# Turning the weighted LoRA projections: TensorE transposes, or VectorE block transposes with ScalarE copies

## The chip, the core and the metric

The kernel runs on one core of a Trainium2 chip. The metric is the device time of one execution in microseconds (us). The engines are named as the profile names them: PE is TensorE's matmul, PEld its weight load, DVE is VectorE, ACT is ScalarE, POOL is GpSimd and SP is SyncE, which issues nearly all DMAs here.

## What is computed

There are 8 samples of 256 tokens and 1024 features, all fp32. Each sample picks one of 8 conditioning matrices, and the result runs through a linear layer with a routed low-rank (LoRA) correction:

```
y      = einsum('bsi,boi->bso', x, weight[adapter_ids])        # 1024 x 1024 per sample
base   = einsum('btd,od->bto', y, base_W) + base_b
probs  = softmax(einsum('btd,nd->btn', y, router_W) + router_b) # n = 15
topk_p, topk_i = top_k(probs, 8);  mapped = expert_map[topk_i]
w      = weight of each of the 8 experts for each token
h      = einsum('btd,erd->bter', y, A)                          # 8 experts x rank 16 = 128
out    = x + base + einsum('bter,eor->bto', h * w[..., None], B) * 2.0
```

The product `h * w` is what the change is about. For one sample it is 256 tokens by 128 expert-rank values. The code calls it `hw`. It is computed with tokens on the partitions, and the last product (`B`) needs it with the 128 expert-rank values on the partitions: it has to be turned.

## The kernel before

**Two stages.** Stage one (lines 251 to 534) makes `y` for one sample after another, 8 rounds of its loop (`b` = 0 to 7). Stage two (lines 539 to 812) makes base and correction for two groups of four samples. Both use a Strassen-like scheme with 7 block products in place of 8: three PSUM accumulators `pa`, `pb`, `pc` collect blocks of several products, with copies and sums in between. In stage one a block is 4 fp32 matmuls of 128x512 (`block`, line 276; the trace shows two passes for each, 8 records). In stage two the scheme is nested: 7 outer products (`seven`) with 7 inner blocks each, per group; `here` counts the outer products from 0 to 13. A block there is 4 matmuls of 128x256 (line 573) and, where the correction is added, 2 more with `hwT` (line 582).

**The order is written by hand.** PE, DVE, ACT and SP run what the code issues, in that order (`manual_schedule`). One round of stage one for a middle sample issues on PE:

- `pa` = a11 b11 (read by an ACT copy at line 452)
- `pb` = a12 b21 (read by DVE at line 457)
- the two transposes of the last round's `hw` (line 247)
- `pc` = s1 t1 (read by an ACT copy at line 482)
- `pa` += s2 t2 (read by an ACT copy at line 484)
- `pc` += s4 b22 (read by DVE at line 464)
- `pa` += the block with a21 (read by DVE at line 470), the projection of the sample before (line 139, `ph`), `pa` += a22 t4 (read by DVE at line 287)

(Counting the transposes out, these are blocks one to seven with the projection ahead of the seventh. In round 7 the order is another: `pa`, `pc` with s1 t1, `pa` with s2 t2, `pb`, the two transposes, then the block with a21, `pc` with s4 b22, and the last.)

The block s1 t1 and the block s4 b22 use the same accumulator `pc`, so the second of them may not write before the ACT copy of line 482 has read it.

**Turning y.** DVE transposes 32x32 blocks in place (`flip`, line 287), and 16 ACT copies (`moves`, line 298) carry 32 partitions each from one quarter of the partitions to another: source quarter `a`, target quarter `r`, `a` running fastest. There are two such sets of 16 per sample; the second one is called `behind` and runs at the start of the next round, 4 copies ahead of the ACT copy of line 452 and 12 behind it.

**The router and hw.** `project(b, ph)` issues 16 matmuls and returns small DVE and ACT steps: `logits`, `softmax`, `top`, `route_to` and `weigh` (line 197), which writes `hw`, one of two places by the sample's parity. In round `b` of stage one it serves sample `b - 1`.

**Turning hw.** `turn` (lines 243 to 248) is called once per sample: in rounds 2 to 7 behind the `pb` block (line 460), and in stage two behind the outer products `here` = 1 and 2 (lines 806 and 812). It issues two PE transposes with an identity into a PSUM tile `pt` and one ACT copy of 128x256 into `hwT` (line 248). The first four samples' `hwT` is first used by the outer product 1, the others' by product 8.

**The head.** Line 421 issues 11 matmuls of the identity with itself into the same `pt`, before the first weights arrive. The pools of PSUM are `ps_t` (1 bank, `pt`), `ps` (6 banks) and `ps_h` or `ps_e` (1 bank).

Of the kernel before, what the change touches and what calls it, by code (L numbers as in the profile page):

```python
# [10 lines left out]
F32 = mybir.dt.float32  # L11
# [17 lines left out]
def kernel(  # L29
# [15 lines left out]
    nc = tc.nc  # L45
    P = 128
    B = ids.shape[1]
    S = 256
    KC = 8
    KH = 4  # L50
    OH = 512
# [5 lines left out]
    GB = 4  # L57
    NTT = S // P
# [4 lines left out]
    wpool = ctx.enter_context(tc.tile_pool(name="w", bufs=8))  # L63

    tpool = ctx.enter_context(tc.tile_pool(name="t", bufs=6))
    ps_t = ctx.enter_context(
        tc.tile_pool(name="ps_t", bufs=1, space=bass.MemoryType.PSUM)
    )
    dram = ctx.enter_context(
        tc.tile_pool(name="scratch", bufs=1, space=bass.MemoryType.DRAM)  # L70
    )
# [12 lines left out]
    ident = const.tile([P, P], F32, name="ident")  # L84
# [9 lines left out]
    hwTs = [const.tile([P, 2, 2, S], F32, name=f"hwT{g}") for g in range(B // GB)]  # L94
# [37 lines left out]
    def project(b, ph, order=(0, 1)):  # L132


        y = yv[b // GB]
        th, bi = b % GB // 2, b % 2
        for j in order:
            for k in range(KC):
                nc.tensor.matmul(  # L139
                    ph[:, j, : ER + N],  # L140
                    lhsT=y[:, k // KH, th, k % KH // 2, bi, k % 2, ts(j, P)],
                    rhs=ar_sb[:, k, :],
                    start=(j == order[0] and k == 0),
                    stop=(k == KC - 1),
                    skip_group_check=True,
                )
        t = places
        hw = t[f"hw{b % 2}"]

        def logits():  # L150
            lg = t["lg"]
            nc.vector.tensor_add(
                lg, ph[:, :, ER : ER + N], rb.unsqueeze(1).to_broadcast([P, NTT, N])
            )
            mx = t["mx"]
            nc.vector.tensor_reduce(mx, lg, AX.X, ALU.max)
            nc.vector.tensor_sub(lg, lg, mx.unsqueeze(2).to_broadcast([P, NTT, N]))
            nc.scalar.activation(t["ex"], lg, AF.Exp)
            nc.scalar.copy(t["h"], ph[:, :, :ER])

        def softmax():
            den = t["den"]
            nc.vector.tensor_reduce(den, t["ex"], AX.X, ALU.add)
            rden = t["rden"]
            nc.vector.reciprocal(rden, den)
            pr = t["pr"]
            nc.vector.tensor_mul(pr, t["ex"], rden.unsqueeze(2).to_broadcast([P, NTT, N]))

        def top():
            pr, first = t["pr"], t["top"]  # L170
            rest = t["rest"]
            for j in range(NTT):
                nc.vector.max(out=first[:, j, :], in_=pr[:, j, :])
            for j in range(NTT):
                nc.vector.match_replace(
                    out=rest[:, j, :],
                    in_to_replace=first[:, j, :],
                    in_values=pr[:, j, :],
                    imm_value=0.0,
                )  # L180

            nc.vector.tensor_sub(t["kept"], pr, rest)

        w = t["w"]

        def route_to(j):
            def run():
                kr = t[f"kr{j}"]
                nc.vector.tensor_mul(
                    kr, route, t["kept"][:, j, :].unsqueeze(1).to_broadcast([P, E, N])  # L190
                )
                nc.vector.tensor_reduce(w[:, j, :], kr, AX.X, ALU.add)

            return run

        def weigh():
            nc.vector.tensor_mul(
                hw.rearrange("p j (e r) -> p (j e) r", r=R),
                t["h"].rearrange("p j (e r) -> p (j e) r", r=R),
                w.rearrange("p j e -> p (j e)").unsqueeze(2).to_broadcast(  # L200
                    [P, NTT * E, R]
                ),
            )

        return [logits, softmax, top, route_to(0), route_to(1), weigh], (b, hw)

# [33 lines left out]

    EN = mybir.EngineType

    def turn(b, hw):

        pt = ps_t.tile([P, S], F32, name="pt")
        for j in range(NTT):
            nc.tensor.transpose(pt[:, ts(j, P)], hw[:, j, :], ident)  # L247
        nc.scalar.copy(hwTs[b // GB][:, b % GB // 2, b % 2, :], pt)


    with ExitStack() as phase:
        xpool = phase.enter_context(tc.tile_pool(name="x", bufs=2))
        prep = phase.enter_context(tc.tile_pool(name="prep", bufs=1))
        ps = phase.enter_context(
            tc.tile_pool(name="ps", bufs=2, space=bass.MemoryType.PSUM)
        )
# [25 lines left out]
                    skip_group_check=True,  # L282
                )

        def flip(half, of):

            nc.vector.transpose(half, of)  # L287

        def moves(b, oh, m):


# [10 lines left out]
                for r in range(4)  # L302
                for a in range(4)
            )

        def run(steps, n=None):
            for _ in range(len(steps) if n is None else min(n, len(steps))):
                steps.popleft()()

        spare = prep.tile([P, 28, P], F32, name="spare")  # L310

# [104 lines left out]
        x, q = load(0)  # L416
        first = q

        idle = ps_t.tile([P, S], F32, name="pt")
        for _ in range(11):  # L420
            nc.tensor.matmul(idle[:, :P], lhsT=ident, rhs=ident, start=True, stop=True)
        t1, t2, t4 = turns(x)
        first_sum(q)
# [3 lines left out]
        waiting = None  # L427
        behind = deque()
        for b in range(B):
# [16 lines left out]
            pb = ps.tile([P, OH], F32, name="pb")  # L446
# [8 lines left out]
            def first_results():  # L455
                block(pb, q["a12"], b21, True)
                nc.vector.tensor_add(m0[:, 0], pb, m0[:, 0])
                flip(m0[:, 0], m0[:, 0])
                if waiting:
                    turn(*waiting)  # L460

            def by_s4():
                block(pc, q["s4"], b22, False)
# [29 lines left out]
            elif not last:  # L493
# [11 lines left out]
                steps, waiting = project(b - 1, ph)  # L505
# [6 lines left out]
            else:  # L512
# [12 lines left out]
                steps, waiting = project(b - 1, ph)  # L525
# [13 lines left out]
    with ExitStack() as phase:  # L539
# [9 lines left out]
        ps = phase.enter_context(  # L549
            tc.tile_pool(name="ps", bufs=2, space=bass.MemoryType.PSUM)  # L550
        )
# [121 lines left out]
        for g in range(B // GB):  # L673
            y, hw = yv[g], hwTs[g]
# [75 lines left out]
            for n, (right, base, into, done, *up_hw) in enumerate(seven):  # L750
                here = g * len(seven) + n
                gaps = {k: [] for k in range(7)}

                if n + 1 < len(seven):
                    follows = seven[n + 1][0]
                else:
                    follows = None if end else yv[g + 1][:, 0, 0]
                steps = [] if follows is None else differences(follows)
                nexts = []


                def advance(n, steps=steps, nexts=nexts):
                    def run():
                        soon.extendleft(
                            (lambda s=s: nexts.append(s())) for s in reversed(steps[n])
                        )

                    return run


                steps = [steps[:2], steps[2:3], steps[3:]]
                for k, m in ((0, 0), (3, 1), (4, 2)):
                    gaps[k].append(advance(m, steps))
                if here == 0:
                    gaps[2].append(lambda: soon.extend(steps_of))
                if n == 0:
                    gaps[1].append(lambda: first_terms((0, 0), (0, 1)))
                    gaps[4].append(lambda: first_terms((1, 0)))
                    gaps[6].append(lambda: first_terms((1, 1)))
                elif n in outer:  # L780
                    gaps[1].append(lambda n=n: soon.extend(outer[n]))
                if n in result_of:
                    for k, ij in enumerate([(0, 0), (1, 1), (0, 1), (1, 0)]):
                        gaps[k].append(lambda r=result_of[n] + ij: load_x(*r))
                if end and n == 6:

                    r = (1, 0, 1, 0)
                    gaps[5].append(
                        lambda: soon.append(lambda: add(u[:, 1, 0], u[:, 1, 0], xs[r]))
                    )  # L790
                if here == 0:
                    for k, count in enumerate((0, 1, 1, 4, 4, 4, 2)):
                        gaps[k].append(lambda count=count: run(behind, count))
                if here + 2 < len(lefts):

                    def fetch(m=here + 2):
                        left[m] = load_left(lefts[m])

                    gaps[5].append(fetch)
                product(  # L800
                    left.pop(here), terms, right, base, into, done, gaps, *up_hw,
                    *([None] * (2 - len(up_hw))), end and n == 6
                )
                terms = nexts
                if here == 1:
                    turn(*waiting)

                    ph = ps_e.tile([P, 2, S], F32, name="pe")
                    steps, waiting = project(B - 1, ph)
                    soon.extend(steps)  # L810
                elif here == 2:
                    turn(*waiting)


# [63 lines left out]
```

## Time and profile before

| what | value |
|---|---|
| median of 3 runs (lowest to highest) | 435.49 us (434.95 to 435.57) |
| the profiled execution, its own time | 435.61 us |
| its span, first to last instruction | 433.8 us |
| PE busy | 428.2 us, 99% of the span |
| PEld busy | 294.7 us, 68% |
| DVE busy | 325.7 us, 75% |
| ACT busy | 138.7 us, 32% |
| TensorE clock granted over the span | 1.00 |
| transposes of line 247 | 16 (2 for each of 8 samples) |
| copies of line 248 | 8, 0.372 us each |
| copies of line 298 | 256, 0.402 us each |

The table is an average over two stages with different loads: in the four rounds from 66.6 to 179.3 us PE is busy all the time, DVE 23.2 us of 28.2 and ACT 15.8 us of 28.2. In stage two ACT has little to do. The chain of waits follows the work that ended last backwards; its lines give start, length, engine and tile. The timelines give for each group of instructions the start, the length, the line, the operation, and in brackets how long the engine idled before it and what ended that.

### The profile page before, as it was taken

The page shows a single profiled execution, that of the slowest core. Times are in us where ns is not written, and L with a number is a line of the kernel's source. Part 1 is how long each engine was busy: PE and PEld are TensorE (multiplying, and loading weights), DVE is VectorE, ACT ScalarE, POOL GpSimd, SP SyncE. Part 2 cuts the span into 40 slices and gives each one's busy share as a digit, 9 for nine tenths or more (in the row PEclk, how much of TensorE's full clock was granted, in tenths as well). Part 3 has the DMA queues.
Part 4 walks back from the last instruction along what each step waited for, and adds up shares of the span by engine and source line. Part 5 has one row for each costly group of instructions (what it writes and reads, how often), then busy time and mean ns, then how long its engine had stood idle before and what let it go on. Part 6 is the DMA issues. An engine that isn't in the chain of part 4 may idle for free.

```text
span 433.8 us, 4826 instructions
## 1 busy us (share of the span) xinstructions
PE 428.2 (99%) x1654; PEld 294.7 (68%) x1654; DVE 325.7 (75%) x548; ACT 138.7 (32%) x338; POOL 0.7 (0%) x6
## 2 busy tenths in 40 slices
PE   8999999999999999999999999999999999999997
PEld 5344454644646446455458898888888888888886
DVE  0699999886878888988886866946597858745595
ACT  1019276662755636736538300000201200000200
POOL 0000000000000000000000000000000000000000
PEclk9999999999999999999999999999999999999999
DMA  7997997859578698891749565522968725912843
GB/s 255 417 366 258 348 338 272 329 231 313 200 289 289 219 336 295 290 306 60 259 199 371 214 208 206 196 96 91 380 216 275 286 68 201 391 58 63 299 163 128
DMA packets 32778, 106.04 MB, mean 244 GB/s; under 512 B 3058, under 2 KB 6898, under 8 KB 29554
## 3 DMA queue, kind: packets, MB, share of 16 engines
q1 hardware_dynamic: 32610, 105.21, 66.7%
q10 hardware_dynamic: 144, 0.52, 0.4%
q8 instruction: 13, 0.21, 0.2%
q14 instruction: 11, 0.09, 0.1%
HBM read 84.49 MB, written 21.23 MB: 244 GB/s over the span
## 4 chain that ended last, share of the span: by engine, by line
PE 96%; DMA 2%; SPq 1%; issue 0%; DVE 0%
PE pa L276 24%; PE pa L573 22%; PE pc L276 13%; PE pc L573 11%; PE pb L276 7%; PE ph L139 6%; PE pb L573 6%; PE pc L582 3%; DMA wt<-in_wq_dram 2%; PE pb L582 2%; PE pa L582 1%; PE pe L139 1%; PE pe L573 1%; PE pt L247 0%; SPq L353 0%; DMA ids_sb<-in_ids_dram 0%
## 5 line engine op out<-in xcount | busy, mean ns | idle before, releaser
L298 ACT COPY y<-late 32x256 f32<-32x256 f32 x256 | 103.0, 402 | 63.2 <-DVE late L287 60.2
L573 PE MATMUL pa<-tt,wt 128*128 128x256 f32 x324 | 78.0, 379 | 0.0
L573 PEld LDWEIGHTS pa<-tt,wt 128*128 128x128 f32 x324 | 61.4, 190 | 8.7 <-DVE q L603 0.3
L276 PE MATMUL pa<-wt,x 128*128 128x512 f32 x128 | 57.7, 593 | 0.6 <-DMA wt<-in_wq_dram 0.6
L276 PE MATMUL pa<-wt,tt 128*128 128x512 f32 x120 | 54.0, 593 | 0.0
L276 PEld LDWEIGHTS pa<-wt,x 128*128 128x128 f32 x128 | 24.1, 190 | 30.7 <-issue 29.9
L276 PEld LDWEIGHTS pa<-wt,tt 128*128 128x128 f32 x120 | 22.3, 190 | 26.1 <-issue 25.9
L612 ACT ACTIVATE q<-pa,bb 128x256 f32<-128x256 f32 x12 | 5.0, 470 | 105.9 <-PE pa L573 105.0
L139 PEld LDWEIGHTS ph<-late,y 128*128 128x128 f32 x224 | 28.4, 189 | 3.3 <-issue 3.3
L276 PE MATMUL pb<-wt,x 128*128 128x512 f32 x64 | 29.1, 595 | 0.6 <-DMA wt<-in_wq_dram 0.6
L276 PE MATMUL pc<-wt,x 128*128 128x512 f32 x64 | 28.9, 594 | 0.0
L276 PE MATMUL pc<-wt,tt 128*128 128x512 f32 x64 | 28.8, 592 | 0.0
L139 PE MATMUL ph<-late,y 128*128 128x143 f32 x224 | 28.6, 284 | 0.0
L573 PE MATMUL pc<-tt,wt 128*128 128x256 f32 x112 | 27.8, 379 | 0.0
L399 DVE TENSOR_TENSOR wt<-wt 128x2048 f32<-128x2048 f32 (+1 forms) x9 | 18.4, 2049 | 8.5 <-PE pa L276 5.9
L573 PE MATMUL pc<-y,wt 128*128 128x256 f32 x96 | 24.0, 379 | 0.0
L573 PE MATMUL pb<-y,wt 128*128 128x256 f32 x96 | 24.0, 379 | 0.0
L276 PEld LDWEIGHTS pb<-wt,x 128*128 128x128 f32 x64 | 12.0, 190 | 16.6 <-issue 14.3
L573 PEld LDWEIGHTS pc<-tt,wt 128*128 128x128 f32 x112 | 21.3, 190 | 2.9
L276 PEld LDWEIGHTS pc<-wt,x 128*128 128x128 f32 x64 | 12.1, 190 | 15.5 <-issue 14.8
L573 PE MATMUL pa<-y,wt 128*128 128x256 f32 x92 | 21.8, 379 | 0.0
L276 PEld LDWEIGHTS pc<-wt,tt 128*128 128x128 f32 x64 | 11.7, 190 | 12.9 <-issue 12.2
(120 smaller groups left out, 531.2 us busy)
## 6 DMA issues: line engine op xcount, KB each, us to landing
wt<-in_wq_dram SPq DMA_DIRECT2D x28, 1024.0 KB, 5.6
wt<-left_raw SPq DMA_DIRECT2D x14, 1024.0 KB, 5.3
wt<-left_sum SPq DMA_DIRECT2D x14, 768.0 KB, 8.4
out_dram<-q SPq DMA_DIRECT2D x31, 256.0 KB, 2.3
x<-in_xq_dram SPq DMA_DIRECT2D x7, 1024.0 KB, 7.0
late<-in_xr_dram SPq DMA_DIRECT2D x20, 256.0 KB, 6.6
wt<-in_wq_dram SPq DMA_DIRECT2D x8, 512.0 KB, 7.8
spare<-in_bq_dram SPq DMA_DIRECT2D x4, 1024.0 KB, 5.3
```

The source lines that it names most:

```text
L139: nc.tensor.matmul(ph[:, j, : ER + N], lhsT=y[:, k // KH, th, k % KH // 2, bi, k % 2, ts(j, P)], rhs=ar_sb[:, k, :], start=(j == order[0] ...
L276: nc.tensor.matmul(acc, lhsT=right[:, k, :], rhs=left[:, k, :], start=(first and k == 0), stop=(k == KH - 1), skip_group_check=True,)
L298: lambda a=a, r=r: nc.scalar.copy(y[32 * r : 32 * r + 32, :, :, a, :], m[32 * a : 32 * a + 32, :, :, r, :])
L399: nc.vector.tensor_add(q["s1"][:, h], q["a21"][:, h], q["a22"][:, h])
L573: nc.tensor.matmul(acc[mi][:, mi, :], lhsT=left[:, 2 * k + mi, :], rhs=right[:, k, :], start=(first and k == 0 and (mi == 0 or acc[0] is n ...
L582: nc.tensor.matmul(acc[mi][:, mi, :], lhsT=up[:, ts(mi, P)], rhs=hw, start=False, stop=True, skip_group_check=True,)
L612: nc.scalar.activation(dst[:, mi], acc[mi][:, mi], AF.Identity, bias=bb[:, c : c + 1])
```

## The change

`turn` no longer uses PE or PSUM. `weigh` gets one more DVE instruction: a transpose of 32x32 blocks of `hw` in place (128x256). `turn` then returns 16 ACT copies of 32 partitions by 2x32 elements, in the same order of quarters as the copies of line 298, and its callers run them all at the places where the transposes and the one copy were issued. The pool `ps_t` goes; the identity matmuls of the head write into a `pb` tile of the pool `ps`, and there are 13 of them in place of 11. `flip` and `run` move out of stage one's block, without change.

```diff
-    ps_t = ctx.enter_context(
-        tc.tile_pool(name="ps_t", bufs=1, space=bass.MemoryType.PSUM)
-    )
...
                     [P, NTT * E, R]
                 ),
             )
+            flat = hw.rearrange("p j f -> p (j f)")
+            flip(flat, flat)
...
+    def flip(half, of):
+
+        nc.vector.transpose(half, of)
+
+    def run(steps, n=None):
+        for _ in range(len(steps) if n is None else min(n, len(steps))):
+            steps.popleft()()
+
     def turn(b, hw):
 
-        pt = ps_t.tile([P, S], F32, name="pt")
-        for j in range(NTT):
-            nc.tensor.transpose(pt[:, ts(j, P)], hw[:, j, :], ident)
-        nc.scalar.copy(hwTs[b // GB][:, b % GB // 2, b % 2, :], pt)
+        to = hwTs[b // GB][:, b % GB // 2, b % 2].rearrange("p (j a t) -> p j a t", j=NTT, a=4)
+        return deque(
+            (
+                lambda a=a, r=r: nc.scalar.copy(
+                    to[32 * r : 32 * r + 32, :, a, :],
+                    hw[32 * a : 32 * a + 32, :, ts(r, 32)],
+                )
+            )
+            for r in range(4)
+            for a in range(4)
+        )
...
-        idle = ps_t.tile([P, S], F32, name="pt")
-        for _ in range(11):
+        idle = ps.tile([P, OH], F32, name="pb")
+        for _ in range(13):
             nc.tensor.matmul(idle[:, :P], lhsT=ident, rhs=ident, start=True, stop=True)
...
                 if waiting:
-                    turn(*waiting)
+                    run(turn(*waiting))
...
                 if here == 1:
-                    turn(*waiting)
+                    run(turn(*waiting))
...
                 elif here == 2:
-                    turn(*waiting)
+                    run(turn(*waiting))
```

More of the change, by code (lines that the diff above doesn't have):

```diff
@@ L283, in block @@
                 )
-        def flip(half, of):
-            nc.vector.transpose(half, of)
         def moves(b, oh, m):
@@ L304, in moves @@
             )
-        def run(steps, n=None):
-            for _ in range(len(steps) if n is None else min(n, len(steps))):
-                steps.popleft()()
         spare = prep.tile([P, 28, P], F32, name="spare")
```

## The prediction

> **What bounds the kernel now.** I read the page's busy times first, then the chain of waits, then the timelines of ACT, PE and DVE around each place where hw is turned. PE is busy 99% of the span and the chain runs through it for 96%:
>
> ```profile
> PE 428.2 (99%) x1654; PEld 294.7 (68%) x1654; DVE 325.7 (75%) x548; ACT 138.7 (32%) x338; POOL 0.7 (0%) x6
> PE 96%; DMA 2%; SPq 1%; issue 0%; DVE 0%
> ```
>
> So a microsecond taken from PE's queue is a microsecond won, unless PE then waits for someone. Other engines matter only where PE already sits close behind them. The chain shows what one turn of hw costs PE (columns: start, length):
>
> ```profile
> 63.85 3.43 PE pb L276 x8
> 67.28 0.22 PE pt L247 x2
> 67.50 3.44 PE pc L276 x8
> ```
>
> The two transposes lie on the chain with 0.22 us. The next view decides the case. It is ACT's timeline in rounds 2 and 3 (start, length, line, operation):
>
> ```profile
> 65.76 4.95 ACT L298 COPY y<-late 32x256 f32<-32x256 f32 x12
> 70.73 0.37 ACT L248 COPY hwT<-pt 128x256 f32<-128x256 f32 x1
> 71.03 0.58 ACT L482 COPY late<-pc 128x512 f32<-128x512 f32 x1
> ...
> 92.72 4.96 ACT L298 COPY y<-late 32x256 f32<-32x256 f32 x12
> 97.70 0.37 ACT L248 COPY hwT<-pt 128x256 f32<-128x256 f32 x1
> 99.20 0.58 ACT L482 COPY late<-pc 128x512 f32<-128x512 f32 x1 [1.12 <-PE pc L276]
> ```
>
> The single hwT copy stands directly ahead of the copy of line 482, and that one frees `pc` for PE's block s4 b22. Round 1, which turns nothing, shows that PE really waits for it:
>
> ```profile
> 45.29 0.58 ACT L482 COPY late<-pc 128x512 f32<-128x512 f32 x1
> 45.93 0.30 PEld L276 LDWEIGHTS pc<-wt,x 128*128 128x128 f32 x2 [0.70 <-ACT late L482]
> ```
>
> ```profile
> 42.62 3.43 PE pa L276 x8
> 46.06 3.57 PE pc L276 x8
> ```
>
> The copy ended at 45.29 + 0.585 = 45.87. PE's block was due at 42.46 (recorded start of the block before) + 3.43 = 45.89 and took 0.14 too long, so it ran as if started at 46.03: 0.16 after the copy's end. This **handover of 0.16 us** is used below.
>
> **Removed.** 8 pairs of transposes at 0.22 = 1.75 us of PE. The 8 hwT copies (0.372) are replaced.
>
> **Added on ACT: 16 copies of 32 partitions x 64 elements per sample.** The trace has no copy of that size. *Length:* the nearest row is line 298, the same kind of copy with 256 elements, 0.402 us. Per element, PSUM copies give (0.585 - 0.372) / 256 = 0.83 ns, so 64 elements take 0.402 - 192 x 0.00083 = 0.242. *Start to start:* 12 copies of line 298 last 4.95, so they start every (4.95 - 0.40) / 11 = 0.414: no overlap, a gap of 0.012. Other ACT pairs do overlap:
>
> ```profile
> 61.22 0.23 ACT L158 ACTIVATE late<-late 128x30 f32<-128x30 f32 x1
> 61.35 0.35 ACT L159 COPY late<-ph 128x256 f32<-128x256 f32 x1
> ```
>
> The second starts 0.13 after the first, which lasts 0.23. So the **pitch** of the new copies lies between 0.242 - 0.095 = 0.147 (overlapping like this pair) and 0.229 (the 30-element Exp) + 34 x 0.00083 + 0.012 = 0.27. I take 0.242 + 0.012 = **0.254**, because the new copies follow the pattern of line 298 exactly: 32 partitions, source quarter changing from copy to copy.
>
> Here the Trainium skill has a rule for either side. "ScalarE: Activation LUTs", section "What ACT_TABLE_LOAD costs", says that back-to-back ACTIVATEs overlap by about 93 ns; the Exp pair agrees (95 ns), line 298 does not (-12 ns). By that rule the pitch is about 0.15 and the sum below about -1.0 us. "VectorE: DVE Perf Modes", section "Two Vector instructions with no wait between them", models a Vector instruction as held until all earlier ones finish when its input or output starts in another quadrant than the last one's. It does not speak of ScalarE. If ScalarE does the same, line 298 is explained, the new copies are held too, and the sum is the +2.0 us below.
>
> **Round 2.** ACT is late here: `behind` waited for DVE until 63.61. New copies from 65.76 + 4.95 + 0.01 = 70.72, 16 x 0.254 later 74.78, copy 482 from 74.80 to 75.38, handover 75.54. PE's block, recorded at 74.20, is due at 74.20 - 0.22 = 73.98. Wait 1.56, less 0.22 saved: **+1.34**.
>
> **Rounds 3 to 6** (a period of 28.17, the same pattern): ACT starts anew behind PE's `pa` (92.11), so lateness does not add up. Copies from 97.69 to 101.75, copy 482 to 102.35, handover 102.51. Due: 102.38 - 0.22 = 102.16. Wait 0.35, less 0.22: +0.13 each, **+0.53**. What is queued behind on ACT: copy 484 is due when s2 t2 ends, about 102.3, and its reader on PE comes a block (3.43) later; the 16 moves behind it wait 4.39 for DVE anyway. Both hide the shift.
>
> **Round 7.** Copies 482 and 484 (ends 212.2) stand ahead of the turn here, and ACT then waits until 224.35 for DVE: the 4.1 us of copies are covered. **-0.22**.
>
> **Added on DVE: 8 block transposes of 128x256.** Line 287 takes 0.711 for 512 elements; less 256 at 1.02 ns ((0.685 - 0.424) / 256, lines 388 and 197) gives 0.45, half of it 0.36. I take 0.45. It waits for `weigh` (dependent pairs there start 0.03 after the end), and the overlap of `weigh` with its follower goes: a shift of 0.42 + 0.03 + 0.45 - 0.08 - 0.33 = **0.49**. In stage one it is covered: in rounds 3 to 6 DVE's wait of 0.51 at line 457 takes it, in round 2 the 0.85 at line 464, after `weigh` of 203 us the 0.80 at line 457. Without that cover it would move the copies of round 2, where PE waits already. In stage two it is not covered:
>
> ```profile
> 240.61 0.42 DVE L197 TENSOR_TENSOR late<-late 128x256 f32<-128x256 f32 x1
> 240.94 0.68 DVE L726 TENSOR_TENSOR y<-y 128x512 f32<-128x512 f32 x1
> ...
> 244.99 0.68 DVE L603 TENSOR_TENSOR q<-pa,u 128x512 f32<-128x512 f32 x1
> ```
>
> DVE runs without a pause here, and PE's next block on `pa` already takes 1.87 where its kind takes 1.73 (chain, 245.86): 244.99 + 0.68 + 0.16 = 245.83 against 245.69. All of the shift lands there: +0.49. Behind the second `weigh` (270.11) the drain of `pa` ends at 271.12 + 0.49, handover 271.77, against a block due at 271.56: +0.21. The same shift lasts to the drain ending at 277.25 + 0.49, handover 277.90, against 277.81: +0.09; then DVE's pause of 0.88 at 282.34 swallows it. Two pairs of transposes save 0.44. The ACT copies of stage two have nobody behind them for 20 us. **Stage two: +0.35**.
>
> **The head: two more identity matmuls.** The last passes of the 11 start every 0.11 us, the last at 5.42; four more passes end their issue by 5.97. The first real matmul waits for a DMA until 6.37, so 0.4 us covers them. Were they at the pace of 0.21 that the passes before 4.9 us show, the first block would start 0.5 late, and PE's wait of 0.57 for DMA at 12.94 would swallow that. Cost 0; no gain either, since the first real matmuls already start every 0.43, full pace. PSUM tiles keep their two buffers.
>
> **Sum:** 1.34 + 0.53 - 0.22 + 0.35 = **+2.0 us**. The profiled execution took 435.61 (span 433.8, 1.8 around it), 0.12 above the median of the runs shown: 435.61 + 2.0 = **437.6**.
>
> The skill's table in "VectorE: DVE Perf Modes", section "Rules for kernel authors", speaks against the change: transpose 128x128 on TensorE if PSUM will do. The rows agree for this place, 0.22 on PE and 0.37 on ACT against 0.49 on DVE and 4.1 on ACT.
>
> **Rivals.** (1) *The copies overlap.* For it speaks the Exp pair. Pitch 0.15: copy 482 of round 2 ends at 73.8, handover 73.94 before 73.98; no wait in rounds 2 to 6. Saved 6 x 0.22 = 1.31, stage two +0.35: -1.0, **434.6**. This is the rival on the other side: each 0.01 of pitch is 0.8 us (5 rounds x 16) down to 0.232, where rounds 3 to 6 stop waiting; from there 0.16, and the sum turns negative at 0.217. Against it: 232 neighbouring copies of line 298 without one overlap. (2) *The copies are held but shorter, and DVE's transpose costs half.* Pitch 0.24 and a shift of 0.40: round 2 waits 1.34 (+1.12), rounds 3 to 6 wait 0.13 (-0.09 each), round 7 -0.22, stage two 0.40 + 0.12 + 0.09 - 0.44 = +0.17; in all +0.7: **436.3**. (3) *ACT's fixed cost is that of the Exp.* Pitch 0.27: 16 x 5 x 0.016 = 1.3 more, **438.9**. (4) *The change does not do what it says,* PE not being freed: the new order of instructions has no line 247 on PE, the other lines stand as before, and the 16 copies replace line 248 in the same places; I give it nothing.
>
> **How the numbers follow.** Forecast (436.6 to 438.4) 0.65, rival 1 0.08, rival 2 and what lies between it and the forecast 0.14, rival 3 and worse 0.13. The range takes in pitch 0.27 and the upper half of rival 2: 435.6 to 439.0, leaving out rival 1 and the outer ends, under 0.2. What a measurement can tell from no change is about 0.2%, 0.9 us: faster 0.06 (most of rival 1), same 0.14, slower 0.80.
>
> **What would show it.** Line 247 gone from PE; the new copies 0.24 long, every 0.25; PE's weight load of the block s4 b22 waiting for ACT in rounds 2 to 6, about 1.5 us in round 2 and 0.3 to 0.4 after it; the round's period 28.3 in place of 28.17; the block at 245.86 near 2.36; head as before. Copies that start every 0.15 would make the forecast wrong, and so would a DVE transpose that hides.

## The result and the profile after

| what | before | changed |
|---|---|---|
| median (lowest to highest) | 435.53 us (434.95 to 435.63) | 437.74 us (437.13 to 438.08) |
| the profiled execution, its own time | 435.61 us | 437.13 us |
| its span | 433.8 us | 435.3 us |
| TensorE clock granted over the span | 1.00 | 1.00 |

The changed kernel is slower: the ratio is 1.0053, with a 95% interval of 1.0040 to 1.0066. That is 2.2 us by the medians and 1.5 us by the two spans. The profiled execution of the changed kernel is the fastest of its six, 0.6 us below their median, and we will see where 0.5 of that is.

The page of the changed kernel, busy times and the chain of waits by engine:

```profile
PE 428.2 (98%) x1642; PEld 293.3 (67%) x1642; DVE 328.7 (75%) x556; ACT 166.7 (38%) x458; POOL 0.7 (0%) x6
...
PE 70%; ACT 13%; DMA 7%; DVE 6%; SPq 2%; issue 2%; ACTq 0%; DVEq 0%
```

PE has 12 records fewer than the 1654 of before (16 transposes gone, two identity matmuls of two passes each come in). Its busy time is the same 428.2 us and its share is smaller: work went and waiting came. ACT gained 120 copies and 28 us. The second line, the chain, must be read with care. PE's share falls from 96% to 70%, but the kernel became only 0.5% slower. The chain is followed back through one releaser at each wait. Once it steps from PE to an ACT copy it walks along ACT's queue, which is full at that place, and all this counts as ACT. The shares tell where PE waits, not for how long.

How long is read from the timelines of rounds 2 and 3. First ACT in the changed kernel (start, length, line, operation; the copy with line 482 before is now at line 488, the one with 484 at 490, and the new copies are at line 255):

```profile
65.25 4.96 ACT L308 COPY y<-late 32x256 f32<-32x256 f32 x12
70.23 4.07 ACT L255 COPY hwT<-late 32x64 f32<-32x64 f32 x16
74.33 0.59 ACT L488 COPY late<-pc 128x512 f32<-128x512 f32 x1
74.81 0.59 ACT L490 COPY late<-pa 128x512 f32<-128x512 f32 x1
...
93.59 4.95 ACT L308 COPY y<-late 32x256 f32<-32x256 f32 x12
98.56 4.06 ACT L255 COPY hwT<-late 32x64 f32<-32x64 f32 x16
102.65 0.59 ACT L488 COPY late<-pc 128x512 f32<-128x512 f32 x1
```

ACT's sequence is the one of before, with 4.07 us of copies where one copy of 0.37 stood. Nothing lies between the groups. In round 2 the copy of line 488 starts 4.10 behind the start of the new copies, where the copy of line 482 started 0.30 behind that of the one copy: 3.8 us late. In round 3 it is 4.09 against 1.50, 1.12 of which ACT had waited: 2.6 us late. Then PE in the same rounds:

```profile
70.05 3.60 PE L290 MATMUL pa<-wt,tt 128*128 128x512 f32 x8
74.96 3.70 PE L290 MATMUL pc<-wt,x 128*128 128x512 f32 x8 [1.32 <-ACT late L488]
78.50 3.60 PE L290 MATMUL pa<-wt,x 128*128 128x512 f32 x8
...
99.59 3.60 PE L290 MATMUL pa<-wt,tt 128*128 128x512 f32 x8
103.29 3.70 PE L290 MATMUL pc<-wt,x 128*128 128x512 f32 x8
106.82 3.60 PE L290 MATMUL pa<-wt,x 128*128 128x512 f32 x8
```

In round 2 the block on `pc` was due at 70.05 + 3.43 = 73.48. Its follower starts at 78.50, so it ran as if started at 78.50 - 3.43 = 75.07: 1.59 late. In round 3 the same sum gives 106.82 - 3.43 - (99.59 + 3.43) = 0.37. That one carries no bracket: a block that ends its wait inside the tail of the one before it shows no idle time, and only the distance of the starts, 3.70 and 3.53 where 3.43 is normal, betrays it. PEld's waits show all of them, rounds 1 to 6 (total, times, longest):

```profile
PEld pc L290 <- ACT late L488: 6.6, 6, 2.1
```

Before, this wait appeared once, in round 1, with 0.7; the other five are new. The weight load runs ahead of the matmuls by some 0.5 us, so 2.1 in round 2 costs PE 1.59.

Stage two, DVE where the first `weigh` (line 194) runs:

```profile
241.84 0.41 DVE L194 TENSOR_TENSOR late<-late 128x256 f32<-128x256 f32 x1
242.29 0.45 DVE L244 STREAM_TRANSPOSE late<-late 128x256 f32<-128x256 f32 x1
242.66 0.65 DVE L732 TENSOR_TENSOR y<-y 128x512 f32<-128x512 f32 x1
...
246.68 0.68 DVE L609 TENSOR_TENSOR q<-pa,u 128x512 f32<-128x512 f32 x1
```

From `weigh` to the drain of `pa` at line 609 DVE takes 4.84 us, 4.38 before: 0.46 more. PE's chain shows who pays (start, length, tile):

```profile
247.42 1.99 PE pa L579 x8
...
273.19 3.63 PE pa L579 x16
...
279.40 1.81 PE pa L579 x8
```

Without a wait these would have 1.73, 3.45 and 1.73. The first one also starts late, after PE idled for 0.32. Reckoned by the start of the next block, as in stage one, the three are 0.59, 0.17 and 0.08 us late, and 0.14 of the first was there before.

### The profile page after: what moved, and what is told of

The parts are those of the page before. It is cut to its first block, busy times and chain, and to the rows that moved or that the text cites. A ratio compares the mean times of both kernels' runs of the same rounds, so it can differ in the third digit from the quotient of the medians.

```text
span 435.3 us, 4931 instructions
## 1 busy us (share of the span) xinstructions
PE 428.2 (98%) x1642; PEld 293.3 (67%) x1642; DVE 328.7 (75%) x556; ACT 166.7 (38%) x458; POOL 0.7 (0%) x6
## 4 chain that ended last, share of the span: by engine, by line
PE 70%; ACT 13%; DMA 7%; DVE 6%; SPq 2%; issue 2%; ACTq 0%; DVEq 0%
PE pa L579 20%; PE pa L290 14%; PE pc L579 10%; ACT y L308 7%; PE pc L290 6%; PE ph L136 5%; PE pb L579 5%; ACT hwT L255 4%; PE pc L588 3%; DMA wt<-in_wq_dram 2%; DMA late<-in_xr_dram 2%; DMA late<-in_ar_dram 2%; PE pb L588 2%; PE pa L588 1%; DVE wt L405 1%
## 5 line engine op out<-in xcount | busy, mean ns | idle before, releaser
L255 ACT COPY hwT<-late 32x64 f32<-32x64 f32 x128 | 31.1, 243 | 7.6 <-DVE late L244 6.1
```

Source lines behind the costliest of these rows:

```text
L255: lambda a=a, r=r: nc.scalar.copy(to[32 * r : 32 * r + 32, :, a, :], hw[32 * a : 32 * a + 32, :, ts(r, 32)],)
```

## The experiments

**The theory** is the prediction's: on ACT, 16 copies that may not overlap stand ahead of the copy that frees `pc`; on DVE, an uncovered transpose stands ahead of a drain that PE waits for. Both cost only because of their place. **Rivals:** ACT's added work costs wherever it stands; the copies are slow for their size and not for their quarters of partitions; the head's edit or DVE's transpose alone makes the difference. Each kernel below is the changed one with the edit shown, unless the text says otherwise. Ratios are to the kernel before on the same chip.

**1. The copies of stage one behind the copy of line 490, rounds 2 to 6.**

```diff
                 flip(m0[:, 0], m0[:, 0])
-                if waiting:
-                    run(turn(*waiting))
...
             nc.scalar.copy(m0[:, 1], pa)
+            if waiting:
+                run(turn(*waiting))
```

> The changed kernel, but in rounds 2 to 6 the 16 copies stand behind the ACT copy of line 484 (of before), where ACT waits over 4 us for DVE, and not ahead of the copy of line 482. Theory (the copies delay the copy that frees pc): no PE wait for ACT in rounds 2 to 6, each round 28.17 - 0.22 = 27.95 us; 6 x 0.22 won, stage two still 0.25 worse: 1.0 to 1.1 us less than the kernel before, ratio about 0.9976. Rival A (the place does not matter; ACT's added load or the missing transposes cost the time otherwise): as the changed kernel, ratio about 1.005. Rival B (VectorE's added transpose costs most): rounds stay at 28.3 and the ratio near 1.004.

Measured: 434.35 us against 435.41, ratio 0.9975 (0.9966 to 0.9984). ACT and PE in round 2 of this kernel (lines 486 and 488 are the copies of 488 and 490):

```profile
70.52 0.59 ACT L486 COPY late<-pc 128x512 f32<-128x512 f32 x1
73.90 0.59 ACT L488 COPY late<-pa 128x512 f32<-128x512 f32 x1 [2.79 <-PE pa L290]
74.51 4.06 ACT L255 COPY hwT<-late 32x64 f32<-32x64 f32 x16
78.88 6.61 ACT L308 COPY y<-late 32x256 f32<-32x256 f32 x16 [0.30 <-DVE late L244]
```

```profile
70.27 3.60 PE L290 MATMUL pa<-wt,tt 128*128 128x512 f32 x8
73.70 3.60 PE L290 MATMUL pc<-wt,x 128*128 128x512 f32 x8
```

The same 16 copies take the same 4.06 us. They now fill a stretch in which ACT would wait for DVE anyway, and PE's blocks follow each other every 3.43. The round takes 27.95 us, the 28.17 of before less the 0.22 of the transposes. So ACT's work costs nothing in these rounds by itself; its place did. By the measured terms of the changed kernel this one should save 6 x 0.22 = 1.31 and keep stage two's 0.26: 435.41 - 1.05 = 434.36, and it measured 434.35.

**2. The same, and in stage two DVE's transposes moved out of `weigh` into `turn`, the second `turn` from behind product 2 to behind product 4.**

```diff
-            flat = hw.rearrange("p j f -> p (j f)")
-            flip(flat, flat)
+            if b < B - 2:
+                flat = hw.rearrange("p j f -> p (j f)")
+                flip(flat, flat)
...
     def turn(b, hw):
...
+        if b >= B - 2:
+            flat = hw.rearrange("p j f -> p (j f)")
+            flip(flat, flat)
...
-                elif here == 2:
+                elif here == 4:
                     run(turn(*waiting))
```

> As e1, and in stage two the 32x32 block transpose of samples 6 and 7 no longer follows the weighing: it is issued with the copies behind the outer product 1 (sample 6) and behind the outer product 4 (sample 7). Theory: the blocks on pa that waited for DVE in stage two lose their added waits of 0.45, 0.17 and 0.08 us; all 8 x 0.22 of the transposes are won: 1.75 us less than before, ratio about 0.996. Rival (stage two's loss is not DVE's transpose): as e1.

Measured: 437.99 us, ratio 1.0047 (1.0031 to 1.0064). The expectation failed. The three waits for DVE are gone (1.86, 3.45 and 1.73 in the chain), but a new one is there. ACT, then PE, at product 5 of this kernel:

```profile
303.89 4.07 ACT L259 COPY hwT<-late 32x64 f32<-32x64 f32 x16 [40.70 <-DVE late L245]
307.97 0.84 ACT L622 ACTIVATE q<-pa,bb 128x256 f32<-128x256 f32 x2
```

```profile
304.34 1.89 PE L583 MATMUL pc<-tt,wt 128*128 128x256 f32 x8
308.86 3.46 PE L583 MATMUL pa<-tt,wt 128*128 128x256 f32 x8 [2.63 <-ACT q L622]
```

In product 5 it is ACT (line 622) and not DVE that empties `pa`, and the 16 copies stand directly ahead of it. The block on `pa` was due at 304.34 + 1.73 = 306.07 and started at 308.86: 2.8 us. It is the change's own mistake in another place, and the expectation overlooked this reader. The block then took 3.46 where its kind takes 1.89 in this view. Three stretches of this kernel (PE, PEld, DVE, ACT and POOL busy, then the granted clock, DMA share, GB/s):

```profile
306.00:308.00 2.00, 0.23 (x2) 0.00 (x0) 0.69 (x1) 1.91 (x9) 0.00 (x0) 1.00 1.05 406
308.00:310.00 2.00, 1.14 (x3) 0.96 (x4) 0.00 (x0) 1.54 (x4) 0.00 (x0) 0.62 1.00 358
310.00:312.00 2.00, 2.00 (x7) 1.61 (x6) 0.00 (x0) 0.00 (x0) 0.00 (x0) 0.53 0.94 364
```

The granted clock falls to 0.53 behind the idle time: 1.6 us more, 4.4 in all. Four of the six executions took 437.96 to 438.50 us at a mean granted clock of 0.996. The two others took 436.52 and 436.69 at 1.00 and 0.999, about what 2.8 us alone would give on the 433.7 of experiment 8.

**3. DVE's transpose alone:** the kernel before, with the transpose behind `weigh` into a tile that nobody reads. PE's transposes and the single ACT copy stay.

```diff
+            nc.vector.transpose(
+                t["h"].rearrange("p j f -> p (j f)"), hw.rearrange("p j f -> p (j f)")
+            )
```

> The kernel before with nothing but one more DVE instruction behind each weighing: the same 128x256 block transpose, written to a place that nobody reads (that of h). PE transposes and the ACT copy stay. Theory: nothing in stage one; in stage two +0.45 at the outer product 1 and +0.17 at 2: about +0.6 us, ratio 1.0014. Rival A (DVE's transpose hides): 1.000. Rival B (it costs in every round of stage one too, 8 x 0.45): +3.6 us, ratio 1.008.

Measured: 436.29 us against 435.41, ratio 1.0015 (1.0006 to 1.0024). From the block that the head's DMA releases to the end of stage one it takes 229.04 - 12.52 = 216.52 us; before, 229.45 - 12.94 = 216.51. So the six transposes of stage one cost nothing. Stage two, in the chain of this kernel:

```profile
245.76 1.99 PE pa L576 x8
...
271.75 1.90 PE pa L576 x8
```

These are the first two of the three waits, worth 0.6 together (0.44 and 0.17). The third is not there: PE's transposes, which stay in this kernel, let the block come later by 0.22. From its first block to the end of the span stage two takes 204.96, 0.61 more than before; the medians differ by 0.9, and the interval of the ratio goes from 0.3 to 1.0 us.

**4. The head with 11 identity matmuls as before.**

```diff
-        for _ in range(13):
+        for _ in range(11):
```

> The changed kernel with 11 identity matmuls in the head, as before the change, in place of 13. Theory (covered by the wait for the first weights): as the changed kernel, ratio to before about 1.005; the DMA landing ends the head at 12.4 to 12.9 us in either. Rival (the two more matmuls delay or help the head): 0.4 to 0.5 us off that, ratio 1.004 or 1.006.

Measured: 437.58 us, ratio 1.0052 (1.0039 to 1.0064): the changed kernel's. The block that waits for the last DMA of the head, here and in the next experiment, which has 13:

```profile
12.89 0.70 PE L290 MATMUL pb<-wt,x 128*128 128x512 f32 x1 [0.52 <-DMA wt<-in_wq_dram]
```

```profile
1.36 5.82 PE L427 MATMUL pb<-ident 128*128 128x128 f32 x26 [1.36 <-POOL ident masks.py:199]
7.02 3.60 PE L290 MATMUL pa<-wt,x 128*128 128x512 f32 x8
...
12.92 0.70 PE L290 MATMUL pb<-wt,x 128*128 128x512 f32 x1 [0.57 <-DMA wt<-in_wq_dram]
```

In the second the identity matmuls ran at the slower pace and the first block started at 7.02, about 0.65 later than in experiment 4 (6.38); the wait for the DMA takes it up. Over all ten profiles the start of the block that waits for the DMA lies between 12.38 and 12.94, with either number of matmuls: 12.94, 12.52 and 12.89 with 11, and 12.43, 12.66, 12.70, 12.92, 12.93, 12.65 and 12.38 with 13.

**5 and 6. Which quarters change from copy to copy.** Experiment 5 exchanges the loops, so that `r` runs fastest: the source quarter stays for four copies, and the target changes each time.

```diff
-            for r in range(4)
             for a in range(4)
+            for r in range(4)
```

> The changed kernel with the two loops over quarters of the 16 copies exchanged: four copies in a row read the same quarter of partitions and write four different ones. Theory 1 (a copy is held until the one before has ended when either its source or its target quarter differs): the pitch stays 0.255, ratio about 1.005. Theory 2 (only a changed source quarter holds): 12 of 16 overlap, pitch 0.15 there, the 16 copies take 2.8 us, ratio about 0.999. Theory 3 (short ACT copies from SBUF to SBUF never overlap): as theory 1.

Experiment 6 reads from the target's own quarter, so that neither changes within four copies. The correction is then summed from wrongly placed values; sizes and number of copies are the same.

```diff
-                    hw[32 * a : 32 * a + 32, :, ts(r, 32)],
+                    hw[32 * r : 32 * r + 32, :, ts(a, 32)],
```

> The changed kernel with source and target quarter exchanged on the reading side: each copy reads the same quarter of partitions that it writes, so 12 of 15 neighbours change neither. The correction is then summed from wrongly placed values; the work is the same in number and size. Theories 1 and 2: those 12 overlap by about 0.09 us, pitch 0.15, the 16 copies take about 2.8 us; rounds 3 to 6 lose their wait, round 2 keeps about 0.3; ratio about 0.999. Theory 3: pitch 0.255 as before, ratio 1.005.

Measured, on one chip: experiment 5 took 437.59 us against 435.66, ratio 1.0046 (1.0029 to 1.0063), experiment 6 434.71 us, ratio 0.9979 (0.9969 to 0.9988). ACT in round 2, first experiment 5, then 6:

```profile
70.74 4.07 ACT L255 COPY hwT<-late 32x64 f32<-32x64 f32 x16
74.83 0.59 ACT L488 COPY late<-pc 128x512 f32<-128x512 f32 x1
```

```profile
70.72 2.76 ACT L255 COPY hwT<-late 32x64 f32<-32x64 f32 x16
73.50 0.58 ACT L488 COPY late<-pc 128x512 f32<-128x512 f32 x1
```

The same copy of 0.243 us starts every 0.255 when a quarter changes and every 0.148 when none does. Experiment 6 holds both cases: the copies within a group of four start every 0.147, and at the three places where the group changes the next one starts 0.25 later. All its copies stay within one quarter from source to target, so a change of quarter from one copy to the next is enough to hold a copy, even when none crosses. With 2.76 us instead of 4.07 PE waits 0.28 in round 2 and not at all in rounds 3 to 6. That is the prediction's rival 1 made real: 434.71 where it said 434.6.

**7. 24 copies instead of 16**, the last eight a second time into the same places.

```diff
-            for r in range(4)
+            for r in (0, 1, 2, 3, 2, 3)
```

> The changed kernel with 24 copies in place of 16 per turn (the last 8 are made twice, into the same places). Theory (PE waits for the ACT queue in rounds 2 to 6): 8 x 0.255 = 2.04 us more in each of 5 rounds, nothing in round 7 and in stage two: 10.2 us over the changed kernel, about 448 us, ratio 1.029. Rival (the copies are mostly covered and the loss lies elsewhere): under 2 us more.

Measured: 450.23 us, ratio 1.0334 (1.0317 to 1.0351). The expectation was 10.2 us over the changed kernel; it became 12.5 by the medians (450.23 - 437.74). One part is on ACT:

```profile
70.45 6.28 ACT L255 COPY hwT<-late 32x64 f32<-32x64 f32 x24
```

The group lasts 2.22 us more, where 2.04 was expected; in five rounds that is 11.1. The rest lies on PE:

```profile
77.40 5.40 PE L290 MATMUL pc<-wt,x 128*128 128x512 f32 x8 [3.54 <-ACT late L488]
...
109.63 3.70 PE L290 MATMUL pc<-wt,x 128*128 128x512 f32 x8 [2.32 <-ACT late L488]
...
201.23 5.26 PE L290 MATMUL pc<-wt,x 128*128 128x512 f32 x8 [2.31 <-ACT late L488]
```

Two of the five late blocks took 5.3 to 5.4 us in place of 3.70, as in experiment 2, at a granted clock of 0.53 and 0.50 in the lowest stretches of 2 us. In this execution (451.62 us, mean clock 0.992) that is 3.3 us beside the 11.1. The other three (449.89 to 450.31 us, 0.996) fit one such block each; they have no profile. So ACT's time ahead of line 488 passes to PE in full, five times, and behind two of the waits PE lost more than the wait itself.

**8. Experiment 2 with the second `turn` behind product 3.**

```diff
-                elif here == 4:
+                elif here == 3:
```

> As e2, but sample 7 is turned behind the outer product 3 and not behind 4, so that the 16 copies end some 9 us ahead of the ACT reads of pa and pc in the outer product 5, which they stood ahead of in e2. Theory (e2 lost its gain because its last 16 copies held up the ACT read of pa that PE waits for, 2.8 us, and the next block then ran at half pace, 1.7 us): no PE wait at the outer product 5, clock 1.00 throughout, all 8 x 0.22 of the transposes won, no waits in stage two: 1.7 us less than before, ratio 0.996, about 0.6 us under e1. Rival (the late block transpose itself costs in stage two): as e2, or no better than e1.

Measured: **433.73 us** against 435.62, ratio 0.9959 (0.9946 to 0.9973): faster than both kernels. In this kernel PE waits for ACT and DVE no more than before the change (chain, then PEld's waits):

```profile
244.00 1.87 PE pa L583 x8
...
269.64 3.45 PE pa L583 x16
```

```profile
PEld pc L294 <- ACT late L490: 0.7, 1, 0.7
...
PEld pa L583 <- DVE q L613: 0.3, 1, 0.3
```

The gain of 1.9 us is, within the interval, what leaves PE: 8 x 0.22 = 1.75.

## Why the prediction was right

It named the bound, the place and the size, and each term has its own measurement. Starts are compared between the two profiled executions; round 7 is counted from its `pc` block and stage two from its first block to the end of the span.

| term | predicted | measured |
|---|---|---|
| round 2 | +1.34 (wait 1.56) | +1.37 (29.54 against 28.17; wait 1.59) |
| rounds 3 to 6 | +0.53 (4 waits of 0.35) | +0.60 (28.32 against 28.17; waits of 0.37) |
| round 7 | -0.22 | -0.22 (24.52 against 24.74) |
| stage two | +0.35 | +0.26 (204.61 against 204.35) |
| head | 0 | -0.51 in this execution |
| sum | +2.0 | +1.50; +2.01 without the head |

That the predicted +2.0 and the measured +2.01 meet so closely is partly luck: rounds 2 to 6 were taken 0.10 too small and stage two 0.09 too large.

- **The pitch of the new copies** was the term on which everything hung. Taken at 0.254 from line 298, measured 0.255; the length, 0.242, measured 0.243. Of the 120 neighbours in the profile none overlap. Experiments 5 and 6 show why line 298 was the row to take and not the overlapping Exp pair: a copy whose source or target quarter differs from the last one's is held until that one ends. In the changed kernel only the source changes within each four copies, in experiment 5 only the target, and none of them overlap: either one is enough. In experiment 6, where neither changes, they overlap.
- The Trainium skill gave a rule for either side, and the runs give each its domain. "VectorE: DVE Perf Modes", section "Two Vector instructions with no wait between them", models the hold for Vector instructions that change quadrant; here ScalarE's copies show the same (0.255). "ScalarE: Activation LUTs", section "What ACT_TABLE_LOAD costs", states an overlap of about 93 ns; the copies that stay in one quarter show it (0.243 - 0.148 = 0.095), the others do not.
- **The handover of 0.16**, read from one place in round 1, held: in round 2 line 488 ends at 74.33 + 0.585 = 74.92 and PE runs as if from 75.07.
- **The covers in stage one** held. Experiment 3 shows DVE's six transposes there at no cost, and the shift of the second copy and of the moves behind it delayed nobody.
- **DVE's transpose** took 0.445 where 0.45 was estimated. The shift at the drain was 0.46 (predicted 0.49) and the three waits 0.44, 0.17 and 0.08 (0.49, 0.21, 0.09). This is the only term that was too large. The ACT copies of stage two had nobody behind them for 18.3 and 31.5 us, where the prediction said 20.
- **The head** costs nothing, as said, but by the second of its two covers. The 0.4 us ahead of the first real block did not cover the added matmuls: that block started at 6.48 in the changed kernel without a wait ahead of it, and at 7.02 in experiment 5, where 6.37 was the start before. The later wait for DMA took this up. The -0.51 belongs to the execution, not to the edit: the DMA of the second half of the weights let the block start at 12.43 instead of 12.94, and experiment 4 puts such differences on both numbers of matmuls. It is why the two spans differ by 1.5 and the medians by 2.2. The remaining 0.2 between the sum and the medians is less than the runs scatter.
- **Rival 1** was the right one to fear: experiment 6 shows that the sign of the result hangs on whether the copies overlap. In rival 2 the prediction kept 0.09 for the third wait of stage two; with its shift of 0.40 that handover comes at 277.81, just when the block is due, and the rival is worth 436.2 and not 436.3. Nothing hangs on it.
- What the prediction did not see is that the same steps in other places (experiment 8) take 4.0 us less (437.74 - 433.73). Each cost came from where a step was issued, and none from the step itself.

## What to carry to other kernels

An engine with two thirds of its time free can still delay the engine that is the bound: what counts is which copy stands behind the new work in its queue, and who waits for that copy. Before adding work to a queue, list for that place the next instruction that frees a buffer for the bound, and put the work behind it and not ahead; do this anew for each place, since in experiment 2 the reader of `pa` in product 5 was another engine than in product 2. For many small copies across partitions take the pitch from a row with the same pattern of partitions, not from a pair that happens to overlap.

## What the runs showed of the hardware

- **These ScalarE copies of 32 partitions overlap, by 0.095 us, only where neither the source nor the target quarter changes from one to the next.** Pitch 0.148 against 0.255 for the same 32x64 copy of 0.243. Whether copies that cross quarters overlap when the quarters stay the same from one to the next, no run shows. In experiment 7 the pitch was 0.267 from the tenth copy on; why is open.
- **Behind a wait of PE the granted clock was sometimes halved.** The block behind an idle time of 3.54, 2.63 and 2.31 us ran at a granted clock down to 0.50 and took 1.6 to 1.7 us more; behind 2.31 and 2.32 us in rounds 3 to 5 of experiment 7, and behind 1.32 in the changed kernel, it did not. The length of the wait does not decide alone. One of the 23 executions of the kernel before that stand beside experiments 1 to 4 took 436.82 us at a mean clock of 0.995, a loss of about that size; it has no profile, so what went before it there is not known. The Trainium skill, "TensorE: Matmul & The Clock Gate", section "What's actually happening", describes a free-running window of about 3.4 us behind the gate, which would make it a matter of where the wait falls in the window; no run here tests that, and the drops behind 2.31 and 2.63 us came with waits shorter than one such window.
- **TensorE or VectorE for turning a tile** was decided by neither one's price. The skill's table in "VectorE: DVE Perf Modes", section "Rules for kernel authors", prefers TensorE for 128x128. It was right for the change as it stood (ratio 1.0053), and experiment 8 (0.9959) shows the contrary for the same instructions in other places: where TensorE is the bound, 0.45 us on DVE and 4.1 us on ACT per sample, both hidden, cost less than 0.22 us on PE.
